# First DFT stage and half-filled depthwise blocks as products on the four quarters of TensorE's array

## The chip, the cores and the metric

The kernel runs on one core of a Trainium2 chip. The metric is the device time of one execution in microseconds; lower is better. TensorE is called PE here, VectorE DVE, ScalarE ACT, GpSimd POOL and SyncE SP, as in the profile.

## The reference

The input is 32 images of 96 channels and 56x56 points, in float32. Two layers follow each other:

- A convolution block: `h = relu(bn(w1 x))` with 576 hidden channels, a 3x3 depthwise convolution on them, again batch norm and ReLU, then `x + bn(w2 h)`.
- On the 3136 tokens of each image: layer norm, `h = relu(bn(w1 t))` with 192 channels, a Fourier transform over the tokens, a complex diagonal product with bias and ReLU on the real and imaginary parts, the inverse transform's real part, a product with `w2`, and the sum with `t`. Then layer norm and a two-layer network of 384 hidden channels whose products are quantized to 8 bits, and the sum with `t`.

```python
X = jnp.fft.fft(h, axis=1, norm='ortho')
xr = relu(X.real * rd - X.imag * idg + rb)
xi = relu(X.imag * rd + X.real * idg + ib)
y = jnp.fft.ifft(xr + 1j * xi, axis=1, norm='ortho').real
```

The transform over 3136 = 56 x 56 tokens is done in two stages of 56 points. This change concerns the first stage, and a part of the depthwise convolution.

## The kernel before

An image is cut into two halves of 28 rows. The 576 hidden channels are four full blocks of 128 and a last block of 64 channels. Each job of the program is a function that makes steps:

- `unit(img, s, k)`, for a half and a full block: PE expands 96 channels to 128 (L582), ACT evicts, DVE runs most of the nine taps (L635), ACT makes one or two taps as products that the POOL queue's DMAs add, ACT applies ReLU (L652).
- `last_channels(img, s)`, for the last 64 channels of a half: the partitions hold 64 channels twice, for even and odd rows, in the tile `hl`. PE does the depthwise convolution itself, as products with `band`, 64x64 diagonal blocks of tap weights. `strip(o, j)` is one of four steps, for the parity `o` of the output row and the slot `j` of the row pair that is read. Each has three column shifts `dc` and two strips of seven row pairs `t`, six matmuls of 128 rows by 64 columns on 7 x 56 points (L727). Output strip `t` lies in the column half 64t of the array. For `j != o` one of the two 64-row blocks of `band` is zero. ACT finishes with ReLU into `al` (L739).
- `front(img, s)` contracts back to 96 channels (L834, L868), keeps the tokens, and starts layer norm. For each of its two quarters of an image `mixer_in` normalizes, turns (L935) and evicts to `xnT` (`turned`, L938), then twice, for four and three of seven groups: `project` (L951), `bend` (ReLU to `z`, L964), `spread` (first DFT stage, L975) and `gather` (copy to `ya`, L986, L990, L991). `send` writes `ya` to `ydr` in DRAM by four DMAs on SP (L1009). In a group 112 partitions hold two image columns of 56 tokens; the matrix `wa` is 112x112 with two 56x56 blocks on its diagonal and zeros elsewhere. There are four `mixer_in` an image.
- `mid(img, half)` loads `ydr` into `yb` (`load`, L1031), does the second DFT stage (L1058), the diagonal product, and the way back to `gdr`, with `half_project` (L1144) and `project` (L1156).
- `back(img, h)` finishes the inverse transform and the quantized network.

All jobs' steps go to one `Plan`. A step names its engine, a cost, the steps it waits for, the buffers that it takes and gives, and a rank. `Plan.emit` runs through time with these costs and sends out, for each engine that is free, the ready step of the lowest rank. So the order of instructions on each engine is fixed when the program is built, and engines work through it in order. `START`, `PACE`, `OFF` and `AT` set ranks; `pe`, `act` and `dve` set costs. Of the buffers, `ps` (PSUM, two banks each) has 3, `z` 2, `ya` 1, `xnT` 1, `hl` one for each half. Their numbers are the counts in `Plan`:

```python
"xt": 1, "norma": 2, "brief": 3, "xnT": 1, "z": 2, "ya": 1, "wb": 1, "yb": 2,
```

Of the kernel before, what the change touches and what calls it, by code (L numbers as in the profile page):

```python
# [46 lines left out]
HF = 384  # L47
SK = 2 * S
NP = S // 2
R = 28  # L50
# [11 lines left out]
def dft_constants():  # L62
# [10 lines left out]
    a1[:, 1, 0] = sign  # L73
    wa = np.zeros((2, S, 2, 2, NP))
    for b in range(2):
        wa[b, :, b] = a1

# [29 lines left out]
    for pair in range(NP):  # L107
# [11 lines left out]
    return {  # L119
        "wa": wa.reshape(SK, SK).astype(np.float32),  # L120
        "wb": wb.reshape(SK, NP * SK).astype(np.float32),
# [7 lines left out]

START = {"last": 9, "front": 7, "mid": 59, "back": 98}  # L130
PACE = {"last": 2.099, "front": 0.4, "mid": 0.675, "back": 0.45}
CHAIN = 0.6

OFF = (-4.0, 1.0, 0.5, 6.5)
AT = (2.5, 1.5)

# [125 lines left out]
def tile_kernel(ctx: ExitStack, tc: tile.TileContext, d: dict, out: bass.AP):  # L262
# [41 lines left out]
    cw = cst([128, 2, 4], "cw")  # L304
    wa = cst([SK, SK], "wa")
    wc = cst([SK, SK], "wc")
# [13 lines left out]
    gd = cst([KD, G, C], "gd")  # L320
    xnT = cst([C + 1, G * SK], "xnT")
    xs_ring = [cst([C, XW], f"xs{j}") for j in range(3)]
# [35 lines left out]
    make_identity(nc, ident)  # L358
    nc.gpsimd.memset(xnT[C : C + 1, :], 1.0)
    nc.gpsimd.memset(band, 0.0)  # L360
# [4 lines left out]
    def loads():  # L365
# [7 lines left out]
        rows = [row(q, n, HA, C + 1) for n in ("a_g1", "a_v1", "a_b1", "a_m1")]  # L373
        load(q, wa, d["wa"])
        yield rows
# [150 lines left out]
    def pe(n, m, passes):  # L526
        return passes * max(0.838 * n, 0.872 * m) / 1000

# [36 lines left out]
    def unit(img, s, k):  # L565
# [95 lines left out]
        for at, q in enumerate(rest):  # L661
            last = q == rest[-1]
            t = step("DVE", dve(W - 28), tap(*q), [t] + c * last, [], ["hs"] * last, rank=4 * n + OFF[2] + at * 3.5 / len(rest))
        if k in DOUBLE:
# [4 lines left out]
    def last_channels(img, s):  # L669
# [44 lines left out]

        def strip(o, j):

            def f():
                if o == j == 0:

                    acc[img, s, NK] = w1.tile([128, RP, S], F32, name="al", bufs=2)  # L720
                    u["d"] = psum()
                pv = u["d"][:, o, 0 : 7 * S].rearrange("p (r c) -> p r c", c=S)
                for dc in (0, -1, 1):
                    ca, cb = max(0, -dc), S - max(0, dc)
                    for t in range(2):
                        at, q = 64 * t, 7 * t + j
                        nc.tensor.matmul(  # L727
                            pv[at : at + 64, :, ca:cb],
                            lhsT=band[:, j, dc + 1, 64 * o : 64 * o + 64],
                            rhs=H[:, q : q + 7, ca + dc : cb + dc],  # L730
                            start=(j == 0 and dc == 0),
                            stop=(j == 1 and dc == 1),
                            skip_group_check=True,
                        )

            return f

        def finish():
# [6 lines left out]

        t = []
        for o in range(2):
            for j in range(2):
                first = ["ps", "al"] if o == j == 0 else []
                t = [step("PE", pe(7 * S, 128, 6), strip(o, j), [a] + t + bands_set, first, [f"hl{s}"] * (o * j))]  # L750
        strips[img, s] = step("ACT", act(14 * S, 1), finish, t, [], ["ps"])
# [64 lines left out]
    def front(img, s):  # L816
# [5 lines left out]
        def conv(i):  # L822

            def f():
                if i == 0:
                    if s == 0:

                        ydr[img] = dram.tile([NP, SK, HA], F32, name="ydr", bufs=4)

                        tdr[img] = dram.tile([2, SK, RP * C], F32, name="tdr", bufs=4)  # L830
                    u["t"] = w1.tile([SK, RP, C], F32, name="xt")
# [62 lines left out]
        for i in range(G):  # L894
            n = min(4, G - i) if i % 4 == 0 else 0
            cost = pe(C, SK, 16) + n * (pe(C, SK, 2) + 0.08)
            if i in (3, 6):
                cost += pe(C, SK, 2 * (i % 4 + 1))
            t = [
                step(  # L900
                    "PE",
                    cost,
                    conv(i),
                    t,
                    ["pw"] * (i % 4 == 0) + ["xt"] * (i == 0) + ["ydr", "tdr"] * (s == 0 and i == 0),
                    (["acc"] * 4 + ["al"]) * (i == G - 1),
                )
            ]
            if i in (3, 6):
                a = i - i % 4  # L910
                ev.append(step("ACT", act((i + 1 - a) * 2 * C), evict(a, i + 1), t, [], ["pw"]))
# [6 lines left out]
    def mixer_in(img, s, j, v, after):  # L918
# [18 lines left out]
        def turned():  # L937
            nc.scalar.activation(  # L938
                xnT[0:C, :].rearrange("p (q w) -> p q w", w=SK), slots(u["ps"])[0:C, 0:G, 0:SK], AF.Copy
            )  # L940
# [4 lines left out]
        def project(i, a, b):  # L945
            def f():
                u["p", i] = psum()
                u["z", i] = w2.tile([SK, 4, HA], F32, name="z")
                pv = u["p", i].rearrange("p j (q w) -> p (j q) w", w=256)
                for q in range(a, b):  # L950
                    nc.tensor.matmul(  # L951
                        pv[0:SK, q - a, 0:HA],
                        lhsT=xnT[:, q * SK : (q + 1) * SK],
                        rhs=watt,
                        start=True,
                        stop=True,
                    )

            return f

        def bend(i, a, b):
            def f():
                pv = u["p", i].rearrange("p j (q w) -> p (j q) w", w=256)
                nc.scalar.activation(u["z", i][:, 0 : b - a, :], pv[0:SK, 0 : b - a, 0:HA], AF.Relu)  # L964

            return f

        def spread(i, a, b):
            def f():
                if i == 0:  # L970
                    u["ya"] = w1.tile([SK, G, HA], F32, name="ya")
                u["y", i] = psum()
                for j, q in enumerate(range(0, b - a, 2)):
                    e = min(q + 2, b - a)
                    nc.tensor.matmul(  # L975
                        u["y", i][0:SK, j, 0 : (e - q) * HA], lhsT=wa, rhs=u["z", i][:, q:e, :], start=True, stop=True
                    )

            return f

        def gather(i, a, b):
            def f():
                ps, ya = u["y", i], u["ya"]
                pv = ps[0:SK, :, 0 : 2 * HA].rearrange("p j (q h) -> p j q h", h=HA)
                if b - a == 4:
                    nc.scalar.activation(  # L986
                        ya[:, a:b, :].rearrange("p (j q) h -> p j (q h)", j=2), ps[0:SK, :, 0 : 2 * HA], AF.Copy
                    )
                else:
                    nc.scalar.activation(ya[:, a : a + 2, :], pv[:, 0, :, :], AF.Copy)  # L990
                    nc.scalar.activation(ya[:, a + 2 : b, :], pv[:, 1, 0 : b - a - 2, :], AF.Copy)  # L991

            return f

        ends = []
        for i, (a, b) in enumerate(HALVES):
            n = b - a
            p = step("PE", pe(HA, SK, 2 * n), project(i, a, b), [t], ["ps", "z"], ["xnT"] * i)
            p = step("ACT", act(n * HA), bend(i, a, b), [p], [], ["ps"])
            p = step("PE", pe(HA, SK, 2 * n), spread(i, a, b), [p] + ends, ["ps"] + ["ya"] * (i == 0), ["z"])  # L1000
            ends = ends + [step("ACT", act(n * HA, 0, 0.05 + 0.05 * i), gather(i, a, b), [p], [], ["ps"])]

        def send():

            yv = ydr[img].rearrange("g (ri b p) h -> ri b g (p h)", ri=2, b=2)
            for b in range(2):
                for ri in range(2):
                    at = b * S + ri * NP
                    nc.sync.dma_start(  # L1009
                        out=yv[ri, b, :, h * G * HA : (h + 1) * G * HA],  # L1010
                        in_=u["ya"][at : at + NP, :, :].rearrange("p q h -> p (q h)"),
                    )
# [4 lines left out]
    def mid(img, half):  # L1017
# [10 lines left out]
        def load(t):  # L1028
            def f():
                u["yb", t] = w2.tile([SK, G, HA], F32, name="yb")  # L1030
                nc.sync.dma_start(  # L1031
                    out=u["yb", t], in_=ydr[img][g0 + G * t : g0 + G * (t + 1)].rearrange("g p h -> p g h")
                )

# [191 lines left out]
    def back(img, h):  # L1226
# [75 lines left out]

        t = step("PE", 0.35, turn, [t], ["ps", "uT"], ["u8"])
        t = step("ACT", act(G * SK), turned, [t], [], ["ps"])
# [37 lines left out]
        for c in range(3):  # L1342
            p = step("PE", 0.35, inner(c), [t], ["ps", "h16"] + ["h8"] * (c == 0), ["uT"] * (c == 2))
            t = p
# [53 lines left out]
        t = step("DVE", 0.34, shift, [t])  # L1398
        t = step("PE", 1.05, total, [t], ["ps", "brief"], ["tt", "y16"])
        t = step("ACT", 0.97, copied_out, [t], [], ["ps"])  # L1400
# [78 lines left out]
```

## Time and profile before

| | us |
|---|---|
| median of 3 runs | 4688.57 (4685.74 to 4690.48) |
| profiled execution, its own time | 4687.61 |
| its span, first to last instruction | 4685.8 |
| PE busy | 4524.5 |
| DVE busy | 4305.0 |
| ACT busy | 4167.4 |
| POOL busy | 339.3 |

The mean granted clock of PE was 0.980. A busy time is the union of an engine's instructions; PE's matmuls are pipelined and their ends are modelled, so what a PE step costs is better read from the start of one step to the start of the next. A float32 matmul of the code is recorded as two instructions ("passes"): L727's 24 matmuls in each of 64 halves are x3072, and L975's four in each of 128 mixers x1024. In a group's row `128*64 128x385` means 128 rows by 64 columns of the array, and 385 moving columns.

### The profile page before, as it was taken

How to read it: one execution, taken by the hardware profiler on the slowest of the kernel's cores; microseconds unless marked ns; L12 is line 12 of the kernel's file. 1: busy time of each engine (PE TensorE's matmuls, PEld its weight loads, DVE VectorE, ACT ScalarE, POOL GpSimd, SP SyncE). 2: the span in 40 equal slices, each digit the busy share in tenths (PEclk: the TensorE clock that was granted, in tenths of full speed). 3: DMA queues.
4: the chain of work that ended last, by engine and by line, in shares of the span. 5: the costliest groups of instructions: out<-in, count | busy, mean ns of one | idle time of the engine just before them, and what ended most of it. 6: DMA issues, size and time to landing. Idle time of an engine off the chain costs nothing.

```text
span 4685.8 us, 83387 instructions
## 1 busy us (share of the span) xinstructions
PE 4524.5 (97%) x32720; PEld 3311.7 (71%) x32720; DVE 4305.0 (92%) x6933; ACT 4167.4 (89%) x5638; POOL 339.3 (7%) x395
## 2 busy tenths in 40 slices
PE   7899999999999999999999999999999999999986
PEld 4566777777777777777777777777777777777774
DVE  8889999999999999999999999999999999999843
ACT  5678899999999999999999999999999999999976
POOL 0100000000000000000000000000000000000000
PEclk7999999999999999999999999999999999999997
DMA  4567876777776777777777777777777777777752
GB/s 96 126 158 164 190 172 168 183 169 176 183 172 170 182 168 177 181 183 165 180 172 175 178 183 171 174 176 173 178 185 167 175 181 170 180 181 167 170 139 78
DMA packets 374994, 789.15 MB, mean 168 GB/s; under 512 B 134052, under 2 KB 234984, under 8 KB 374600
## 3 DMA queue, kind: packets, MB, share of 16 engines
q1 hardware_dynamic: 319144, 479.17, 37.8%
q0 software_dynamic: 55296, 304.64, 33.2%
q8 instruction: 258, 4.23, 0.4%
q14 instruction: 136, 1.11, 0.1%
q10 hardware_dynamic: 160, 0.01, 0.0%
HBM read 286.40 MB, written 192.68 MB: 102 GB/s over the span
## 4 chain that ended last, share of the span: by engine, by line
PE 78%; DMA 8%; ACT 6%; DVE 5%; issue 2%; SPq 0%; ACTq 0%; POOL 0%; DVEq 0%; POOLq 0%
PE pw L834 17%; PE ps L582 13%; DMA gdr<-gc 6%; PE ps L727 6%; PE ps L975 6%; PE ps L951 6%; PE ps L1058 5%; DVE acc L635 3%; PE ps L1257 3%; PE ps L1156 3%; PE ps L1354 2%; PE pw L868 2%; PE ps L684 2%; PE ps L1313 2%; PE ps L935 2%
## 5 line engine op out<-in xcount | busy, mean ns | idle before, releaser
L635 DVE SCALAR_TENSOR_TENSOR acc<-hs,wdw,acc 128x1540 f32<-128x1540 f32 (+2 forms) x1664 | 2972.5, 1794 | 21.9 <-ACT acc L608 9.7
L582 PE MATMUL ps<-xs,w1T 96*128 96x406 f32 x2048 | 821.7, 524 | 15.6 <-ACT hs L592 7.2
L834 PE MATMUL pw<-w2T,acc 128*112 128x96 f32 x7168 | 792.9, 264 | 5.5 <-ACT acc L652 5.4
L834 PEld LDWEIGHTS pw<-w2T,acc 128*112 128x112 f32 x7168 | 755.5, 179 | 50.4 <-issue 26.2
L624 ACT ACTIVATE product<-hs,wdw 128x1568 f32<-128x1568 f32 (+1 forms) x384 | 613.8, 1599 | 15.8 <-DMA product<-product 15.7
L592 ACT ACTIVATE hs<-ps,b 128x812 f32<-128x812 f32 x512 | 482.4, 943 | 153.9 <-PE ps L582 132.4
L727 PE MATMUL ps<-hl,band 128*64 128x385 f32 (+1 forms) x3072 | 551.7, 499 | 2.8 <-ACT hl L707 2.8
L582 PEld LDWEIGHTS ps<-xs,w1T 96*128 96x128 f32 x2048 | 362.5, 192 | 242.9 <-issue 150.8
L643 POOL DMA_DIRECT2D acc<-product x256 | 221.5, 865 | 3646.2 <-DVE acc L635 553.3
L608 ACT ACTIVATE acc<-hs,bd,wdw 128x1568 f32<-128x1568 f32 x256 | 435.3, 1700 | 2.1
L652 ACT ACTIVATE acc<-acc 128x1568 f32<-128x1568 f32 x256 | 386.5, 1510 | 27.2 <-DMA acc<-product 27.1
L727 PEld LDWEIGHTS ps<-hl,band 128*64 128x64 f32 x3072 | 204.7, 137 | 286.7 <-issue 281.6
L1274 ACT ACTIVATE u<-tt,mf,rf 112x96 fp8e5<-112x96 f32 x896 | 347.0, 460 | 10.2 <-DVE mf L810 10.1
L951 PE MATMUL ps<-watt,xnT 97*112 97x192 f32 x1792 | 336.9, 332 | 3.2 <-ACT xnT L938 0.9
L975 PE MATMUL ps<-z,wa 112*112 112x384 f32 (+1 forms) x1024 | 337.0, 451 | 3.1 <-ACT z L964 3.0
L1337 ACT ACTIVATE h<-h 128x784 fp8e5<-128x784 f16 x384 | 331.1, 864 | 9.5 <-DVE h L1331 9.4
L1058 PEld LDWEIGHTS ps<-wb,yb 112*128 112x128 f32 (+1 forms) x3584 | 311.6, 167 | 39.5 <-issue 18.7
L951 PEld LDWEIGHTS ps<-watt,xnT 97*112 97x112 f32 x1792 | 297.1, 179 | 53.0 <-ACT y L1363 18.1
L1058 PE MATMUL ps<-wb,yb 112*128 112x112 f32 (+1 forms) x3584 | 326.1, 272 | 3.6 <-issue 2.3
L1325 ACT ACTIVATE h<-ps 128x784 f16<-128x784 f32 x384 | 315.9, 825 | 9.5 <-PE ps L1313 9.4
L1331 DVE TENSOR_SCALAR h<-h,b1q 128x784 f16<-128x784 f16 x384 | 160.7, 419 | 116.8 <-ACT h L1325 116.3
L975 PEld LDWEIGHTS ps<-z,wa 112*112 112x112 f32 x1024 | 175.3, 177 | 125.2 <-issue 29.2
(148 smaller groups left out, 6514.7 us busy)
## 6 DMA issues: line engine op xcount, KB each, us to landing
acc<-product POOLq DMA_DIRECT2D x256, 784.0 KB, 7.1
product<-product POOLq DMA_DIRECT2D x128, 756.0 KB, 10.6
ydr<-ya SPq DMA_DIRECT2D x512, 147.0 KB
yb<-ydr SPq DMA_DIRECT2D x128, 588.0 KB
wd<-in_wd_dram SPq DMA_DIRECT2D x128, 349.1 KB
wb<-in_wb_dram SPq DMA_DIRECT2D x64, 686.0 KB
xs<-in_x_dram SPq DMA_DIRECT2D x64, 609.0 KB
tdr<-xt SPq DMA_DIRECT2D x64, 588.0 KB
```

The source lines that it names most:

```text
L582: nc.tensor.matmul(u[h][:, j, 0:QW], lhsT=w1T[:, 128 * k : 128 * (k + 1)], rhs=xs[img, s][0:C, at : at + QW], start=True, stop=True,)
L592: nc.scalar.activation(flat[:, 2 * h * QW : 2 * (h + 1) * QW].rearrange("p (j w) -> p j w", j=2), u[h][:, :, 0:QW], AF.Relu, bias=b1[:, k ...
L608: nc.scalar.activation(acc[img, s, k], u["hs"][:, o + up : o + up + R, :], AF.Identity, scale=weight(up, 0), bias=bd[:, k : k + 1],)
L624: nc.scalar.activation(u["p", dr][:, ra:rb, :], u["hs"][:, ra + o + dr : rb + o + dr, :], AF.Copy, scale=weight(dr, 0))
L635: nc.vector.scalar_tensor_tensor(dst, src, weight(dr, dc), dst, ALU.mult, ALU.add)
L652: nc.scalar.activation(acc[img, s, k], acc[img, s, k], AF.Relu)
L727: nc.tensor.matmul(pv[at : at + 64, :, ca:cb], lhsT=band[:, j, dc + 1, 64 * o : 64 * o + 64], rhs=H[:, q : q + 7, ca + dc : cb + dc], star ...
L834: nc.tensor.matmul(u["pw"][0:SK, t, n % 4, 0:C], lhsT=src[rows, (G * t + n) * SK : (G * t + n + 1) * SK], rhs=rhs, skip_group_check=True, **k,
L951: nc.tensor.matmul(pv[0:SK, q - a, 0:HA], lhsT=xnT[:, q * SK : (q + 1) * SK], rhs=watt, start=True, stop=True,)
L975: nc.tensor.matmul(u["y", i][0:SK, j, 0 : (e - q) * HA], lhsT=wa, rhs=u["z", i][:, q:e, :], start=True, stop=True)
L1058: nc.tensor.matmul(o, lhsT=lhsT, rhs=u["wb"][:, G * s + q, :], start=True, stop=True)
L1274: nc.scalar.activation(u["u8"][:, q, :], u["t"][:, q, :], AF.Identity, scale=u["r"][:, q : q + 1], bias=u["m"][:, q : q + 1], saturate=False,)
```

## The change

In `last_channels` four steps become three. `strip(o)` now does the products with `j == o` alone, in which both 64-row blocks are filled. The products with `j != o` are made on the filled 64-row block alone, by a new step `edges`: 12 matmuls of 64 rows by 64 columns, with row half `o` and column half `t`, so that four neighbours in the order lie on the four quarters of the array.

In `mixer_in` both halves are projected and bent first. Then one `spread` does all groups with a 56x64 `wa` that is stored for each row half: the two image columns `b` lie on row halves (partitions 64b to 64b+55), and the first and second part of the groups, `c`, on column halves. It makes 8 matmuls of 384 columns; the second part has three groups, so its first slot is filled with a repeat. Two `gather`s copy 120 partitions by 768. For this `xnT` has 128 columns a group with zeros between its two image columns, `project` uses 120 of them, and `z` and `ya` have 120 partitions. `ydr` is laid out with the real and imaginary parts outermost; `send` writes 56 rows of 768 or 576 numbers in each of its four DMAs, and `load` in `mid` takes two DMAs of 56 partitions instead of one of 112. Some ranks and costs of the plan change. No instruction of DVE is added or removed.

```diff
-START = {"last": 9, "front": 7, "mid": 59, "back": 98}
-PACE = {"last": 2.099, "front": 0.4, "mid": 0.675, "back": 0.45}
+START = {"last": 9, "front": 7, "mid": 62, "back": 98}
+PACE = {"last": 3.023, "front": 0.4, "mid": 0.54, "back": 0.45}
-OFF = (-4.0, 1.0, 0.5, 6.5)
-AT = (2.5, 1.5)
+OFF = (-4.5, 0.5, 0.5, 8.5)
+AT = (3.0, 0.5)
...
-    nc.gpsimd.memset(xnT[C : C + 1, :], 1.0)
+    nc.gpsimd.memset(wa[:, S:], 0.0)
+    nc.gpsimd.memset(xnT[0:C, :, S:64], 0.0)
+    nc.gpsimd.memset(xnT[C : C + 1, :, :], 1.0)
...
-        return passes * max(0.838 * n, 0.872 * m) / 1000
+        return passes * max(0.855 * n, 0.88 * m) / 1000
...
+        def tap(o, j, t, dc, rows=slice(None), **k):
+            pv = u["d"][64 * t : 64 * t + 64, o, 0 : 7 * S].rearrange("p (r c) -> p r c", c=S)
+            ca, cb = max(0, -dc), S - max(0, dc)
+            q = 7 * t + j
+            nc.tensor.matmul(
+                pv[:, :, ca:cb],
+                lhsT=band[rows, j, dc + 1, 64 * o : 64 * o + 64],
+                rhs=H[rows, q : q + 7, ca + dc : cb + dc],
+                skip_group_check=True,
+                **k,
+            )
...
                 for dc in (0, -1, 1):
                     for t in range(2):
+                        tap(o, o, t, dc, start=(dc == 0), stop=False)
...
+        def edges():
+            for dc in (0, -1, 1):
+                for t in range(2):
+                    for o in range(2):
+                        tap(o, 1 - o, t, dc, slice(64 * o, 64 * o + 64), start=False, stop=(dc == 1))
...
-        for o in range(2):
-            for j in range(2):
-                first = ["ps", "al"] if o == j == 0 else []
-                t = [step("PE", pe(7 * S, 128, 6), strip(o, j), [a] + t + bands_set, first, [f"hl{s}"] * (o * j))]
+        t = step("PE", pe(7 * S, 128, 6), strip(0), [a] + bands_set, ["ps", "al"])
+        t = step("PE", pe(7 * S, 128, 6), strip(1), [t])
+        t = [step("PE", pe(7 * S, 128, 6), edges, [t], [], [f"hl{s}"])]
...
+        def spread():
+            u["ya"] = w1.tile([PK, 2, 4, HA], F32, name="ya")
+            for b in range(2):
+                u["y", b] = psum()
+            for j in range(2):
+                for b in range(2):
+                    at = slice(64 * b, 64 * b + S)
+                    for c in range(2):
+                        z = u["z", c]
+                        rhs = z[at, 2 * j - c : 2 * j - c + 2, :] if c == 0 or j else z[at, 0:1, :].to_broadcast([S, 2, HA])
+                        n = 64 - 8 * c
+                        nc.tensor.matmul(
+                            u["y", b][64 * c : 64 * c + n, j, 0 : 2 * HA], lhsT=wa[at, 0:n], rhs=rhs, start=True, stop=True
+                        )
...
             p = step("PE", pe(HA, SK, 2 * n), project(i, a, b), [t], ["ps", "z"], ["xnT"] * i)
-            p = step("ACT", act(n * HA), bend(i, a, b), [p], [], ["ps"])
-            p = step("PE", pe(HA, SK, 2 * n), spread(i, a, b), [p] + ends, ["ps"] + ["ya"] * (i == 0), ["z"])
-            ends = ends + [step("ACT", act(n * HA, 0, 0.05 + 0.05 * i), gather(i, a, b), [p], [], ["ps"])]
+            ends.append(step("ACT", act(n * HA), bend(i, a, b), [p], [], ["ps"]))
+        p = step("PE", pe(2 * HA, 64, 4), spread, ends, ["ps", "ps", "ya"], ["z", "z"])
+        ends = [step("ACT", act(4 * HA), gather(b), [p], [], ["ps"]) for b in range(2)]
...
-            yv = ydr[img].rearrange("g (ri b p) h -> ri b g (p h)", ri=2, b=2)
+            yv = ydr[img].rearrange("ri g (b p) h -> b (ri g) (p h)", b=2)
             for b in range(2):
-                for ri in range(2):
-                    at = b * S + ri * NP
+                for c in range(2):
+                    at = (h * G + 4 * c) * HA
                     nc.sync.dma_start(
-                        out=yv[ri, b, :, h * G * HA : (h + 1) * G * HA],
-                        in_=u["ya"][at : at + NP, :, :].rearrange("p q h -> p (q h)"),
+                        out=yv[b, :, at : at + (4 - c) * HA],
+                        in_=u["ya"][64 * c : 64 * c + S, b, c:4, :].rearrange("p q h -> p (q h)"),
...
-                nc.sync.dma_start(
-                    out=u["yb", t], in_=ydr[img][g0 + G * t : g0 + G * (t + 1)].rearrange("g p h -> p g h")
-                )
+                for ri in range(2):
+                    nc.sync.dma_start(
+                        out=u["yb", t][S * ri : S * (ri + 1), :, :],
+                        in_=ydr[img][ri, g0 + G * t : g0 + G * (t + 1)].rearrange("g p h -> p g h"),
+                    )
```

## The prediction

> **What bounds the kernel now.** I read the page's busy times first, then the windows over the three stages of the run, then the chain and the PE timeline.
>
> ```profile
> span 4685.8 us, 83387 instructions
> PE 4524.5 (97%) x32720; PEld 3311.7 (71%) x32720; DVE 4305.0 (92%) x6933; ACT 4167.4 (89%) x5638; POOL 339.3 (7%) x395
> PE 78%; DMA 8%; ACT 6%; DVE 5%; issue 2%; SPq 0%; ACTq 0%; POOL 0%; DVEq 0%; POOLq 0%
> ```
>
> Three engines are near full, PE the fullest, and 78% of the chain is PE work. An average over the whole run hides the fill and the tail, so I cut it into windows (span, then busy us of PE, PEld, DVE, ACT, POOL, then granted clock, DMA share, GB/s):
>
> ```profile
> 0.00:585.00 585.00, 517.57 (x3303) 361.60 (x3305) 525.42 (x694) 422.01 (x494) 49.15 (x64) 0.92 0.65 147
> 585.00:4446.00 3861.00, 3829.38 (x28184) 2811.24 (x28180) 3681.04 (x5901) 3576.94 (x4857) 290.14 (x331) 1.00 0.74 175
> 4446.00:4686.00 240.00, 177.53 (x1240) 138.86 (x1237) 98.54 (x339) 168.46 (x290) 0.00 (x0) 0.82 0.41 112
> ```
>
> The middle row decides. In 3861 us PE is busy 99.2%, DVE 95.3%, ACT 92.6%: PE sets the pace, and DVE stands only 180 us behind it. One image takes 140.3 us there (the chain shows the same L684 step at 2101.09 and at 2241.37), so the stretch holds 27.5 images. Per image: PE 139.1 us, DVE 133.8, ACT 130.0.
>
> The operations that change, in groups and then in the PE timeline (start, length, passes; a float32 product is recorded as two passes):
>
> ```profile
> L727 PE MATMUL ps<-hl,band 128*64 128x385 f32 x2048 | 378.3, 491 | 0.0
> L727 PE MATMUL ps<-hl,band 128*64 128x392 f32 x1024 | 224.9, 517 | 2.8 <-ACT hl L707 2.8
> L975 PE MATMUL ps<-z,wa 112*112 112x384 f32 x768 | 295.3, 493 | 3.1 <-ACT z L964 3.0
> L975 PE MATMUL ps<-z,wa 112*112 112x192 f32 x256 | 62.4, 325 | 0.0
> ```
>
> ```profile
> 2016.22 1.45 PE L975 MATMUL ps<-z,wa 112*112 112x384 f32 x4
> 2017.51 1.71 PE L1058 MATMUL ps<-wb,yb 112*128 112x112 f32 x14
> ...
> 2020.37 1.72 PE L834 MATMUL pw<-w2T,acc 128*112 128x96 f32 x16
> 2022.02 1.03 PE L868 MATMUL pw<-w2T,al 64*112 64x96 f32 x16
> 2022.98 1.63 PE L582 MATMUL ps<-xs,w1T 96*128 96x406 f32 x4
> 2024.45 1.13 PE L975 MATMUL ps<-z,wa 112*112 112x384 f32 x4
> ```
>
> Lengths overlap, so cost is read from start to start. The first L975 step takes 2017.51 - 2016.22 = 1.29 us for 4 passes of 384 columns (0.322 each). The second (2 passes of 384, 2 of 192) works out to 0.97. L868, on two 64-row halves in turns, needs 0.96 us for 16 passes where L834 needs 1.65 for 16 on the whole array: halves already run side by side. So do L727's two 64-column halves: the chain gives 2.10 us to a step of 12 passes, though each pass is recorded with 0.49, and 4.05 to two steps in a row.
>
> **What the Trainium skill says.** "TensorEngine Tiling (Array Packing)", Key Properties: tiles load weights and multiply independently, and a change of the tiling mode drains the engine. The trace agrees on both for two tiles: the L868 and L727 figures above, and a drain seen as 2 x 2.10 - 4.05 = 0.15 us for one more entry and exit. "TensorE: Matmul & The Clock Gate", Part 3: row and column tiling compose. No run here shows four 64x64 quarters yet; this is the main unknown. The tiling page's Gotcha 1: row tiles must write different PSUM banks. The change does so (output row parity `o` in strips and image half `b` in spread each have a bank of their own). Part 1 of the TensorE page: a PE with idle windows is clocked at half rate. The trace shows 0.92 in the fill and 0.82 in the tail, but still 1.00 between 468 and 585 us, where PE was busy 112.47 of 117 us (96%).
>
> **The change part by part.**
>
> Strips (64 in the run, two an image). Before: four steps of 12 passes, 4 x 2.03 = 8.1 us. The products with band slot j != o use half of the rows alone. After: `strip(0)` and `strip(1)`, 2.03 each, and `edges`, 24 passes on quarters. If four run at once that is 6 rounds of 0.33 us = 2.0. Saved: 2.03, **4.05 us an image**, on PE, which is the path. One switch to quarters comes in, one step goes: even.
>
> Spread (128, four an image). Before 1.29 + 0.97 = 2.26 us. After: 8 products = 16 passes of 384 columns, 4 rounds of 0.322 = 1.29, and a mode entered and left that was not before, 0.15. Saved 0.82, **3.3 us an image**. Of the 16 slots two are repeats of `z` slot 0; they are counted.
>
> PE in all: 4.05 + 3.3 = 7.35 us an image, 5.3% of its work; 202 us in the middle stretch, so PE needs 3829 - 202 = 3627 there.
>
> ACT: three `gather` copies (103.1 + 64.2 + 44.0 = 211.3 us in the run, rows of L986, L990, L991) become two of 768 columns, 256 x 0.805 = 206. Gain 5 us, beside other work. `bend` and `turned` move the same free sizes (0.80 + 0.65, and 0.83). DVE: no instruction added or removed, 6,936 in both orders.
>
> Weights of `project` grow from 112 to 120 columns. Its pace is set by the 192 moving columns (8 passes in 1.32 us on the chain, 0.165 each; L834 shows 0.103 a pass with 112-column weights), so nothing; uncovered, at most 0.007 x 14 passes x 4 = 0.4 us an image.
>
> DMA: `send` still issues four on SP, but 56 rows of 3072 or 2304 bytes in place of 28 of 5376: 112 more pieces a mixer, 14,336 in all. The hardware queue's 37.8% of 16 engines over 319,144 packets is 89 ns each; at that price, too high since the bytes stay, 80 us an engine, under 2% on a share of 74%. `load` in `mid` becomes two DMAs: 128 issues of 0.42 us on SP, 54 us, while SP waits for ACT on `gc` alone 832 us. Behind them in SP's queue stand the later loads; 0.42 us of delay is covered by the wait. At the start one more constant load and two memsets on POOL (a row of 784 took 0.75 us), 1 or 2 us if nothing covered them, taken as nothing.
>
> The added wait: `spread` now waits for both `bend`s and takes two of the three `ps` buffers at once, while before the first half's spread ran when its own `bend` was done. Behind it in PE's fixed order stand products of other images, and ACT waits for those. The planner ranks it later, with other steps between `project` and `spread`. I price the wait at 0; PE's idle time at L975 was 3 us in the whole run, in nearly the same place. If the cover goes, a `bend` takes 0.80 us and two in turn 1.45; times four, 5.8 us an image would be lost.
>
> **What is late next.** PE at 3627 is now below DVE at 3681, with ACT at 3572. So the saving cannot be had whole: DVE becomes the bound. Its floor is 3681 plus the gaps under 0.3 us that even a fed DVE shows; summed over the trace's DVE instructions in this stretch, 31 us: 3712, a gain of 149. With three engines within 3% of one another each waits for the others; PE alone in front reached 99.2%, but three abreast I put at 97.5% for the first: 3681/0.975 = 3775, **86 us less**. The fill was at 90% DVE and the tail has few of these steps: 10 us together (0 to 20). Sum: 96. The profiled execution took 4687.6 (its span 4685.8 and 1.8 around it), the median of three is 4688.6; so 4592. Ends of this case: 4687.6 - 149 - 20 = 4518, and with DVE at 96.2% (35 us gained, the fill none) 4652.
>
> **Rivals.**
> (a) *Waits replace the work*: the two `ps` buffers and the later `spread` give PE bubbles of about 1.5 us per spread, 6 us an image, so all but 1.35 us of the 7.35 go: 27.5 x 1.35 = 37 us gained, 4651, and up to 4690 if the fill and the tail lose as much. For it: three `ps` buffers in all. Against: `half_project` already takes two at once, and L1144 behind it waited 1.2 us in the whole run.
> (b) *Quarters run only two at a time*, slower: then `edges` takes 12 rounds, 3.96 us, and saves nothing, and `spread` 8 rounds, 2.58 + 0.15 = 2.73, is 0.47 slower than before: 128 x 0.47 = 60 us on the bound engine, 4748. It decides from a round of four of 0.59 us in place of 0.32 (with t for the round, an image saves 2 x (4.05 - 6t) + 4 x (2.11 - 4t), which is zero there). For it: never seen here; each float32 product brings two passes for one quarter, which could hold up the queue. Against: the pairs of L727 also have two passes each and still lose nothing. Wholly in turn it would be 24 x 0.33 and 16 x 0.32, above 5000.
> (c) *The clock falls* since PE now idles: at 0.97, PE needs 3627/0.97 = 3739, still under 3775; it takes perhaps 20 us: 4612, inside the first case.
>
> **How the numbers follow.** First case with (c): 0.79, 4592, 4518 to 4652. (a) 0.09, half of it slightly faster, the rest split over no change and slower. (b) 0.10 at 4748, and 0.02 for something worse. Within 0.2% (9 us, about what this measurement can tell from no change) 0.04. Faster 0.83, slower 0.13. The range runs from 4518 to 4680, which takes in most of (a).
>
> **What would show it.** Right: the 24 passes of `edges` last about 2 us from start to start and the 16 of `spread` 1.3 to 1.45; PE busy falls by roughly 200 us in the middle while DVE's share there rises to 97% or more; the image period is near 137 us. Wrong: `edges` near 4 us (b); or short steps with PE idle before L582 or `spread`, named as waiting for ACT on `ps` or `z` (a); or a clock under 0.97 in the middle (c).

## The result and the profile after

The changed kernel takes 4693.35 us in the median of four runs (4682.55 to 4699.67), the kernel before 4687.15 in the same comparison: a ratio of 1.0012, with a 95% interval of 0.9991 to 1.0033. That is no change. The forecast was 4592 us, a gain of 2%. The profiled execution took 4682.55 us, its span 4680.7.

First the page, with the chain of work that ended last in its third line, then the windows over the same stretches as before:

```profile
span 4680.7 us, 85686 instructions
PE 4397.9 (94%) x33744; PEld 3205.3 (68%) x33744; DVE 4299.8 (92%) x6933; ACT 4170.2 (89%) x5510; POOL 337.3 (7%) x397
PE 46%; ACT 14%; DVE 11%; DMA 6%; issue 2%; SPq 0%; POOLq 0%; ACTq 0%; DVEq 0%
```

```profile
0.00:585.00 585.00, 506.78 (x3473) 357.25 (x3474) 536.08 (x709) 429.55 (x491) 49.46 (x67) 0.89 0.65 149
585.00:4446.00 3861.00, 3715.77 (x29058) 2711.43 (x29056) 3667.61 (x5891) 3576.51 (x4744) 287.87 (x330) 0.99 0.73 175
4446.00:4681.00 235.00, 175.36 (x1218) 136.64 (x1216) 96.07 (x334) 164.18 (x278) 0.00 (x0) 0.79 0.39 107
```

PE's work has gone down: 127 us of busy time over the run, 114 in the middle stretch. Nothing took it up. In the middle PE is now busy 96.2%, DVE 95.0% and ACT 92.6%; DVE and ACT stand where they stood before. PE's idle time there rose from 32 us to 145. The chain that ended last was 78% PE; now it is 46% PE, with ACT and DVE in it at 14 and 11. The new shares add up to 79%, because the chain could be followed back only to about 930 us; of the part that was followed PE has some 58%. So the chain changes from engine to engine. The granted clock of PE fell as well, in every stretch.

The quarters themselves do what was forecast. In PE's timeline (start, length, passes) `edges` and one of the `spread`s:

```profile
2055.57 2.18 PE L722 MATMUL ps<-hl,band 64*64 64x392 f32 x24
2057.68 1.20 PE L1369 MATMUL ps<-h,w2q 128*96 128x392 fp8e5 x6
...
2017.07 1.52 PE L994 MATMUL ps<-z,wa 56*64 56x384 f32 x16
2018.51 1.81 PE L844 MATMUL pw<-w2T,acc 128*112 128x96 f32 x16
```

From start to start `edges` takes 2057.68 - 2055.57 = 2.11 us for 24 passes, and `spread` 2018.51 - 2017.07 = 1.44 for 16. Four quarters run at once.

The wait that the change added is in the same timeline, where a bracket gives the idle time before a row and who ended it:

```profile
2064.22 0.86 PE L994 MATMUL ps<-z,wa 56*64 56x384 f32 x4
2065.79 1.50 PE L994 MATMUL ps<-z,wa 56*64 56x384 f32 x12 [0.71 <-ACT hs L594]
```

```profile
PE ps L1369 <- ACT h L1352: 33.1, 24, 3.8
PE ps L963 <- DVE V L1102: 31.4, 25, 2.6
PE ps L994 <- ACT hs L594: 18.2, 20, 2.4
```

The first two matmuls of this `spread` went into one PSUM buffer; the third, which opens the second buffer, had to wait until ACT had emptied it of another unit's expansion. The second fence is the table of waits (total, times, longest). This wait left PE idle 20 times, 18.2 us in the run. That is not all of it: the quarters of the first buffer go on while those of the second one wait, and then no idle time shows. From the first product of a `spread` to the first one into the second buffer, the starts are 58.8 us apart in all, over the 126 of the 128 steps that show both; 58 of them are over 0.1 us late. That is some 1.8 us an image. It is one of many waits, none of which alone explains the missing 2%.

### The profile page after: what moved, and what is told of

It is laid out like the page before. It is cut to its first block, busy times and chain, and to the rows that moved or that the text cites. A ratio compares the mean times of both kernels' runs of the same rounds, so it can differ in the third digit from the quotient of the medians.

```text
span 4680.7 us, 85686 instructions
## 1 busy us (share of the span) xinstructions
PE 4397.9 (94%) x33744; PEld 3205.3 (68%) x33744; DVE 4299.8 (92%) x6933; ACT 4170.2 (89%) x5510; POOL 337.3 (7%) x397
## 4 chain that ended last, share of the span: by engine, by line
PE 46%; ACT 14%; DVE 11%; DMA 6%; issue 2%; SPq 0%; POOLq 0%; ACTq 0%; DVEq 0%
PE pw L844 10%; PE ps L584 8%; DVE acc L637 7%; DMA acc<-product 5%; PE ps L722 4%; PE ps L1073 3%; PE ps L994 2%; PE ps L963 2%; PE ps L1369 2%; PE ps L1272 2%; PE ps L1171 2%; ACT acc L654 2%; PE ps L1328 2%; ACT product L626 1%; ACT acc L610 1%
## 5 line engine op out<-in xcount | busy, mean ns | idle before, releaser
L584 PE MATMUL ps<-xs,w1T 96*128 96x406 f32 x2048 | 823.4, 526 | 48.8 <-ACT al L751 11.6
L844 PEld LDWEIGHTS pw<-w2T,acc 128*112 128x112 f32 x7168 | 766.4, 181 | 64.3 <-issue 40.3
L844 PE MATMUL pw<-w2T,acc 128*112 128x96 f32 x7168 | 804.9, 267 | 5.0 <-ACT acc L654 4.8
L584 PEld LDWEIGHTS ps<-xs,w1T 96*128 96x128 f32 x2048 | 371.2, 195 | 300.0 <-issue 136.0
L594 ACT ACTIVATE hs<-ps,b 128x812 f32<-128x812 f32 x512 | 478.6, 935 | 97.8 <-PE ps L584 83.2
L654 ACT ACTIVATE acc<-acc 128x1568 f32<-128x1568 f32 x256 | 386.9, 1512 | 63.8 <-DMA acc<-product 63.5
L722 PE MATMUL ps<-hl,band 128*64 128x385 f32 (+3 forms) x3072 | 419.3, 498 | 4.5 <-ACT hs L594 2.3
L963 PE MATMUL ps<-watt,xnT 97*120 97x192 f32 x1792 | 350.3, 341 | 44.3 <-DVE V L1102 31.4
L963 PEld LDWEIGHTS ps<-watt,xnT 97*120 97x120 f32 x1792 | 305.2, 190 | 105.4 <-DVE V L1102 40.2
L722 PEld LDWEIGHTS ps<-hl,band 128*64 128x64 f32 (+1 forms) x3072 | 154.7, 135 | 204.1 <-issue 168.8
L994 PE MATMUL ps<-z,wa 56*64 56x384 f32 (+1 forms) x2048 | 242.6, 510 | 24.3 <-ACT hs L594 18.2
L1328 PE MATMUL ps<-uT,w1q 96*128 96x392 fp8e5 x768 | 196.9, 341 | 26.5 <-ACT xnT L948 9.5
```

What stands on the lines that cost most here:

```text
L584: nc.tensor.matmul(u[h][:, j, 0:QW], lhsT=w1T[:, 128 * k : 128 * (k + 1)], rhs=xs[img, s][0:C, at : at + QW], start=True, stop=True,)
L594: nc.scalar.activation(flat[:, 2 * h * QW : 2 * (h + 1) * QW].rearrange("p (j w) -> p j w", j=2), u[h][:, :, 0:QW], AF.Relu, bias=b1[:, k ...
L654: nc.scalar.activation(acc[img, s, k], acc[img, s, k], AF.Relu)
L722: nc.tensor.matmul(pv[:, :, ca:cb], lhsT=band[rows, j, dc + 1, 64 * o : 64 * o + 64], rhs=H[rows, q : q + 7, ca + dc : cb + dc], skip_grou ...
L844: nc.tensor.matmul(u["pw"][0:SK, t, n % 4, 0:C], lhsT=src[rows, (G * t + n) * SK : (G * t + n + 1) * SK], rhs=rhs, skip_group_check=True, **k,
L963: nc.tensor.matmul(pv[0:PK, q - a, 0:HA], lhsT=xnT[:, q, 0:PK], rhs=watt, start=True, stop=True,)
```

## The experiments

**Theories.** (1) The order of instructions, which the planner writes once and every engine follows, sets the time: after the change it has engines waiting for one another in turn, so that none is full. (1b) The half clock takes PE's saving back: PE idles, is clocked down, and needs longer. (2) DVE, now the fullest engine after PE, is the bound. (3) The `spread`'s wait for two of three PSUM buffers is the bound. The plain rival is that PE is still the bound.

| | us, median | ratio to before (95%) | PE clock |
|---|---|---|---|
| changed kernel | 4693.35 | 1.0012 (0.9991 to 1.0033) | 0.967 |
| old plan constants | 4781.14 | 1.0196 (1.0175 to 1.0217) | 0.955 |
| without `edges` | 4722.72 | 1.0062 (1.0047 to 1.0077) | 0.955 |
| without one tap | 4660.15 | 0.9933 (0.9912 to 0.9954) | 0.970 |
| `edges` on all rows | 4764.79 | 1.0151 (1.0128 to 1.0175) | 0.971 |
| changed kernel, reordered | 4570.36 | 0.9748 (0.9734 to 0.9763) | 0.976 |
| kernel before, reordered | 4730.13 | 1.0088 (1.0073 to 1.0103) | 0.981 |
| strips alone | 4780.10 | 1.0197 (1.0172 to 1.0222) | 0.967 |
| first DFT stage alone | 4875.41 | 1.0400 (1.0381 to 1.0419) | 0.960 |
| reordered, without one tap | 4568.63 | 0.9745 (0.9730 to 0.9759) | 0.977 |
| reordered, `edges` on all rows | 4683.66 | 0.9991 (0.9982 to 1.0000) | 0.978 |
| reordered, without `edges` | 4574.38 | 0.9744 (0.9713 to 0.9774) | 0.971 |
| reordered, without both | 4539.46 | 0.9661 (0.9630 to 0.9692) | 0.972 |

**Old plan constants.** The same work, ordered with the constants of before.

```diff
-START = {"last": 9, "front": 7, "mid": 62, "back": 98}
-PACE = {"last": 3.023, "front": 0.4, "mid": 0.54, "back": 0.45}
-OFF = (-4.5, 0.5, 0.5, 8.5)
-AT = (3.0, 0.5)
+START = {"last": 9, "front": 7, "mid": 59, "back": 98}
+PACE = {"last": 2.099, "front": 0.4, "mid": 0.675, "back": 0.45}
+OFF = (-4.0, 1.0, 0.5, 6.5)
+AT = (2.5, 1.5)
# and pe's and dve's costs as before
```

> The changed kernel with the quarter products as they are, but the plan's constants (START, PACE, OFF, AT, and the PE and DVE costs) of the kernel before. The same instructions, in another order. Theory 1, the order made by the planner sets the time, since no engine is full: slower than the changed kernel by 1 to 3%, 4740 to 4830 us. Theory 2, DVE or ACT is the bound as an engine: within 0.5% of the changed kernel, 4670 to 4715 us. Theory 3, the wait of the spread for two of three PSUM buffers sets the time: within 1%.

Measured: 4781.14 us, inside the range of theory 1 and outside those of 2 and 3. Constants that move no work move the time by 1.9%, about as much as the whole gain that was forecast.

**Without `edges`.** The order is left alone; PE loses work: 11 of the 12 products of `edges` are left out, and the sums of the last 64 channels stay incomplete.

```diff
                     for o in range(2):
-                        tap(o, 1 - o, t, dc, ...)
+                        if dc == 0 and t == 0 and o == 0:
+                            tap(o, 1 - o, t, dc, ...)
```

> The changed kernel in the same order, but the step edges makes one of its 12 products (the depthwise sums of the last 64 channels are left incomplete): some 64 x 1.9 = 120 us of PE work less. Theory 1 (order and waits between the engines): under 40 us faster, 4650 to 4695 us. Theory 1b, the half clock gives PE's savings back: no gain either, and the granted clock falls further, to 0.955 or less. Rival, PE is still the bound: 80 to 120 us faster, 4575 to 4610 us.

Measured: 4722.72 us. The work taken away is 81 us and not 120: from start to start all strip and edge products of the run take 407.7 us in the changed kernel and 326.7 here, as the one product that stays takes some 0.9 us alone. With that much less to do the program is slower than the changed kernel (ratios 1.0062 and 1.0012, intervals that do not meet), and the clock is down to 0.955. PE's work as the bound is out. Theory 1b had said no gain and a clock of 0.955 or less, and both came; that it would even be slower no theory had said. The same stretch, 585 to 4320 us, of the changed kernel and of this one:

```profile
585.00:4320.00 3735.00, 3594.24 (x28096) 2622.64 (x28095) 3551.88 (x5697) 3461.09 (x4586) 279.10 (x320) 0.99 0.73 175
```

```profile
585.00:4320.00 3735.00, 3545.06 (x26729) 2594.60 (x26726) 3518.48 (x5655) 3434.58 (x4546) 278.31 (x318) 0.98 0.73 174
```

PE's idle time rises from 141 to 190 us, and the clock falls from 0.99 to 0.98: 1% of 3735 us is some 37 us of PE time lost there.

**Without one tap.** DVE loses work, a tenth of it: one of the nine taps of every unit is left out.

```diff
-                nc.vector.scalar_tensor_tensor(dst, src, weight(dr, dc), dst, ALU.mult, ALU.add)
+                if (dr, dc) != (0, -1):
+                    nc.vector.scalar_tensor_tensor(dst, src, weight(dr, dc), dst, ALU.mult, ALU.add)
```

> The changed kernel in the same order, but every unit leaves out one of its depthwise taps on DVE (column shift -1 in the same row): 256 x 1.73 = 443 us of DVE work less, 10%. Theory 1 (order and waits): under 100 us faster, 4600 to 4690 us. Theory 2 (DVE is the bound): DVE's floor falls to 3860 us, so PE or ACT must bind next: 200 us faster or more, 4490 us or less.

Measured: 4660.15 us, some 33 us less than the changed kernel, for 418 us less of DVE's busy time (4299.8 to 3881.9). DVE as an engine is not the bound; theory 2 is out.

**`edges` on all rows.** PE gets the work back that the quarters of the strips had saved.

```diff
-                        tap(o, 1 - o, t, dc, slice(64 * o, 64 * o + 64), start=False, stop=(dc == 1))
+                        tap(o, 1 - o, t, dc, start=False, stop=(dc == 1))
```

> The changed kernel in the same order, but edges uses all 128 rows again, the zero half included: its 24 passes then run two at a time, 4.05 instead of 2.1 us, 64 x 1.95 = 125 us of PE work given back. Theory 1: PE's idle time takes up most of it, under 60 us slower, 4690 to 4750 us. Rival, PE is still the bound: 100 to 125 us slower, about 4810 us.

Measured: 4764.79 us, 71 more than the changed kernel for 125 us of work. That lies between the two ranges. So PE's steps are on the path in places. A reading that fits this run and the one without `edges`: a step that becomes longer shifts what follows, while one that becomes shorter leaves a gap, since the next in line waits for another engine.

**Reordered.** The decisive experiment: every instruction of the changed kernel, in another order.

```diff
-START = {"last": 9, "front": 7, "mid": 62, "back": 98}
-PACE = {"last": 3.023, "front": 0.4, "mid": 0.54, "back": 0.45}
-AT = (3.0, 0.5)
+START = {"last": 8.5, "front": 7, "mid": 62, "back": 98}
+PACE = {"last": 3.627, "front": 0.3845, "mid": 0.5416, "back": 0.45}
+AT = (5.0, 1.0)
...
-            t = step("DVE", dve(W - 28, 0.16), tap(*q), ...
+            t = step("DVE", dve(W - 28, 0.1), tap(*q), ...
```

> The changed kernel, the same instructions in another order: START last 8.5, PACE last 3.627, front 0.3845, mid 0.5416, AT (5, 1), and 0.10 us for the fixed part of a DVE tap in the plan's costs. The set was found by replaying orders with the step times that the traces of before and after show, which puts an image at 133.0 us instead of 137 to 139. Theory 1 (order): 90 to 170 us faster than the changed kernel, 4520 to 4600 us, and DVE busy 97% or more of the middle. Rival, the gain is held back by something no order can lift (DMA, half clock, contention): 4650 us or more.

Measured: 4570.36 us, 2.5% faster than the kernel before. This version beats both. Its window from 585 to 4320 us:

```profile
585.00:4320.00 3735.00, 3650.97 (x28898) 2662.76 (x28899) 3644.19 (x5862) 3550.03 (x4714) 286.82 (x329) 1.00 0.75 180
```

PE is busy 97.8%, DVE 97.6%, ACT 95.0%, and the clock is back at 1.00. What has changed is how regularly the images follow. ACT's timeline shows one eviction of `hl` for each half; every second one, in the changed kernel and then in the reordered one:

```profile
2100.18 0.91 ACT L705 ACTIVATE hl<-ps,b 128x784 f32<-128x784 f32 x1
...
2240.67 0.91 ACT L705 ACTIVATE hl<-ps,b 128x784 f32<-128x784 f32 x1
...
2385.69 0.90 ACT L705 ACTIVATE hl<-ps,b 128x784 f32<-128x784 f32 x1
...
2525.31 0.91 ACT L705 ACTIVATE hl<-ps,b 128x784 f32<-128x784 f32 x1
```

```profile
2121.78 0.90 ACT L705 ACTIVATE hl<-ps,b 128x784 f32<-128x784 f32 x1
...
2257.89 0.90 ACT L705 ACTIVATE hl<-ps,b 128x784 f32<-128x784 f32 x1
...
2393.93 0.90 ACT L705 ACTIVATE hl<-ps,b 128x784 f32<-128x784 f32 x1
...
2529.32 0.90 ACT L705 ACTIVATE hl<-ps,b 128x784 f32<-128x784 f32 x1
```

The images are 140.5, 145.0 and 139.6 us apart in the first, 136.1, 136.0 and 135.4 in the second.

The order itself shows the difference more sharply. Take PE's steps, by their lines, from each such eviction to the next. In the kernel before and in the reordered one this sequence is exactly the same for every image from the sixth on: the planner has settled into a repeating order. In the changed kernel no two neighbouring images have the same sequence; in the middle some 78% of the steps agree, laid side by side as well as they fit. With the old plan constants it is 60%; with the strips alone and the first DFT stage alone, which follow below, it is 61 and 66%.

**The kernel before, reordered**, as a fair counterpart.

```diff
-OFF = (-4.0, 1.0, 0.5, 6.5)
-AT = (2.5, 1.5)
+OFF = (-4.0, 0.5, 0.5, 11.0)
+AT = (3.0, 3.0)
...
-        return passes * max(0.838 * n, 0.872 * m) / 1000
+        return passes * max(0.845 * n, 0.88 * m) / 1000
...
-            cost = pe(C, SK, 16) + n * (pe(C, SK, 2) + 0.08)
+            cost = pe(C, SK, 16) + n * (pe(C, SK, 2) + 0.13)
```

> The kernel before, the same instructions in another order: OFF (-4, 0.5, 0.5, 11), AT (3, 3), PE costs 0.845 and 0.88, 0.13 for the start of a group in front. It was the best found in the same way. Theory 1: PE needs 136 us an image by its measured step times and bounds this form, so an order can give little: 4630 to 4680 us. Rival, the kernel before was held back by its order just as much: under 4600 us, and then the quarters give nothing of their own.

Measured: 4730.13 us, a miss by theory 1's numbers: 0.9% slower than the order it had. The replay that chose this order was 50 us and more too hopeful here. The rival, under 4600, is further off. This order repeats too, from the seventh image on, so a repeating order alone is not yet a good one. The best order of the old form that was run stays its own, with PE busy 99.2% in the middle; that none is better is not shown.

**Each half of the change alone**, with the constants of before: `last_channels` of the changed kernel in the kernel before, and then `mixer_in`, `send` and `load` in it.

```diff
# strips alone
-        t = []
-        for o in range(2):
-            for j in range(2):
-                first = ["ps", "al"] if o == j == 0 else []
-                t = [step("PE", pe(7 * S, 128, 6), strip(o, j), ...)]
+        t = step("PE", pe(7 * S, 128, 6), strip(0), [a] + bands_set, ["ps", "al"])
+        t = step("PE", pe(7 * S, 128, 6), strip(1), [t])
+        t = [step("PE", pe(7 * S, 128, 6), edges, [t], [], [f"hl{s}"])]
# first DFT stage alone: the other parts of the change, these four lines as before
```

> The kernel before with the quarter products of last_channels alone, its plan's constants unchanged: 64 x 2.1 = 134 us of PE work less than before. Theory 1: the old constants fit the old steps, the new ones fall out of the repeating order, 4740 to 4840 us, slower than before. Rival, PE's saving counts: 4560 to 4640 us.

> The kernel before with the quarter products of the first DFT stage alone, its plan's constants unchanged: 128 x 0.82 = 105 us of PE work less, and the spread that waits for both halves and takes two PSUM buffers. Theory 1: out of the repeating order, 4770 to 4850 us. Theory 3, the wait for the two PSUM buffers is what eats the gain: slower than strips alone by 50 us or more, with PE idle before the spread. Rival, PE's saving counts: 4590 to 4650 us.

Measured: 4780.10 and 4875.41 us. The strips alone wait for nothing new and use no more PSUM, take some 133 us of work from PE, and cost 2.0%; theory 3 can't explain that, theory 1 can. The first DFT stage alone costs 4.0%, 25 us beyond what was expected for theory 1. It is 95 us slower than the strips, as theory 3 asks; but theory 3 also asks that PE stand idle before the `spread`, and it hardly does. The group of that product in this run, its idle time after the second bar:

```profile
L986 PE MATMUL ps<-z,wa 56*64 56x384 f32 x1024 | 228.8, 503 | 11.6 <-ACT o L1396 5.6 <-ACT uT L1303 2.3 <-ACT hs L594 1.1
```

PE is idle 11.6 us before the `spread`, and the products into the second buffer start late by 37 us in all, in a program that is 185 us slower than the kernel before. Theory 3 in its plain form falls. That holding two buffers delays other users of PSUM, which then wait elsewhere, isn't excluded.

**What binds the good order?** The same three edits on the reordered kernel, and two of them together.

> The reordered changed kernel (4570 us) in its order, with the same one tap of DVE left out in every unit: 256 x 1.73 = 443 us of DVE work less. If DVE as an engine is what bounds the good order (it is busy 97.6% there), 70 to 130 us are gained until PE and ACT bind, 4440 to 4500 us. If the fixed order with its waits binds here too, about 40 us, as in the order given with the change: 4520 to 4540 us.

> The reordered changed kernel in its order, with edges on all 128 rows: 64 x 1.95 = 125 us of PE work given back. If DVE bounds the good order, PE's slack takes most of it: under 50 us slower, 4570 to 4620 us. If PE's steps lie on the path, 70 to 125 us slower, 4640 to 4695 us.

> The reordered changed kernel in its order, with one of the 12 products of edges alone (sums of the last 64 channels incomplete): some 120 us of PE work less, as in the second run, but in the good order. If PE's steps are the path there, 50 to 110 us faster, 4460 to 4520 us. If idle windows and the half clock take back what PE saves, as in the order given with the change, no gain or slower, 4560 to 4610 us, with a granted clock under 0.97.

> The reordered changed kernel in its order, with both left out: 11 of 12 products of edges (120 us of PE work) and one DVE tap in every unit (443 us). Either alone gave nothing. If PE and DVE bound it together, each hiding the other, 50 to 110 us faster, 4460 to 4520 us. If a third thing stands at 136 us an image (ACT, its DMA-added products, or chains through all engines in the fixed order), under 30 us faster, 4540 to 4580 us.

Measured: without the tap 4568.63 us, no gain from 418 us less of DVE's busy time; either theory had forecast at least 30. With `edges` on all rows 4683.66, 113 us more for 125 us of PE work: PE stands close to the bound here. Without `edges` (79 us less work from start to start) 4574.38 us, no gain either; the clock fell to 0.971, but not under the 0.97 named. Without both 4539.46 us, 31 less, just past the edge of the range for a third thing at 136 us an image. That third thing is not found: ACT, the DMA-added products that it waits for, or chains through all engines remain. There is a lead. The chain that ended last, by lines, in the reordered kernel and in the one without both:

```profile
DMA acc<-product 11%; DVE acc L637 9%; PE pw L844 9%; PE ps L584 6%; PE ps L722 5%; PE ps L963 4%; PE ps L1073 3%; ACT acc L610 3%; ACT acc L654 3%; ACT h L1352 3%; PE ps L994 2%; ACT hs L594 2%; ACT ya L1000 2%; PE ps L1369 1%; PE ps L945 1%
DMA acc<-product 11%; PE pw L846 9%; DVE acc L638 7%; PE ps L584 6%; PE ps L965 3%; PE ps L1075 3%; ACT acc L610 3%; ACT acc L655 3%; ACT u L1291 3%; PE ps L723 2%; ACT h L1354 2%; PE ps L996 2%; ACT product L626 2%; ACT hs L594 2%; ACT ya L1002 2%
```

The transfer that adds a product to `acc` stands first in all five runs of this order except those without the tap alone and without `edges` alone, where it is second, always with about 11%; it had 1% of the span before the change and 5% after it. No run changed it, so that it binds is not shown. What is shown is that DVE's 97.6% is not what binds, and that in either order taking work from one engine gives little or nothing.

## Why the prediction was wrong

**Bound before**: right. PE set the pace, and `edges` on all rows costs nearly its full length where the order is good.

**Saving on PE**: right for a step that nothing disturbs, too large for the run. `edges` takes 2.11 us (said: 2.0), and a strip step standing alone 2.10, so a half of an image saves about 2.1 us; an undisturbed `spread` takes 1.44, as said, and saves 0.82. Rival (b), two at a time, is refuted: where the page "TensorEngine Tiling (Array Packing)" of the Trainium skill says in Key Properties that tiles work independently, the trace agrees for four 64x64 quarters of float32, with 24 passes in 2.11 us. But 7.35 us an image would be 235 us in 32 images, and PE's busy time fell by 127. From start to start, idle time left out, the strips save 133 us in the run (said: 130), `spread` 62 (said: 105), `project` takes 21 more (said: nothing), and the remaining steps, which did not change, take some 47 more at the lower clock. In the reordered kernel PE's busy time fell by 174.

**What is late next**: this is the step that failed. "Three abreast I put at 97.5% for the first" is a share of busy time that DVE did not reach: 95.0% was measured. It took the order of instructions for something that adapts. It does not: it is written when the program is built, from ranks and costs, and the order that came with the change kept DVE near its 95.3% of before and brought PE down to 96.2%. In another order the same instructions reach 97.6% and 4570 us, 22 us from the number forecast. So the number 97.5% is met in a good order, and the error lay in granting it to this one. That it is met there is partly luck, since its reason, that DVE becomes the bound, also fell: a tenth of DVE's work less changes nothing there.

**The added wait, priced at 0**: 18.2 us of idle time in the table of waits, and 58.8 us by the late starts, some 1.8 us an image; in the reordered kernel the late starts come to 32 us. So a price of nothing was wrong. The mechanism of rival (a) exists, and its end, about 4690 us, is where the kernel came out; but that is luck: the PE bubbles are spread over many places, not some 6 us an image at the `spread`, and the strips alone, with the constants of before, lose time without that wait.

**The clock**, rival (c): 0.99 in the middle instead of 1.00, inside what (c) allowed, and 0.967 in all instead of 0.980; 1.3% of the span is 61 us of PE time. It was taken for a cost of 20 us beside a gain. It belongs to the lost gain. Three programs with the same instructions bound its part: reordered, changed and with the old constants they have clocks of 0.976, 0.967 and 0.955, and PE is busy 4350.2, 4397.9 and 4450.3 us in them. So of the 114.5 us between the spans of the first two at most 48 are the same PE work taking longer, and 67 are more idle time. What causes what was not separated: no run held the one and changed the other, and in the reordered kernel's middle PE was idle less (84 us instead of 141 in the 3735) while the clock was at 1.00.

**Nothing for DMA, SP and the wider weights**: DVE's and ACT's busy times are the same to within 0.2%, as said. But `project`, with the wider weights, takes 19 us more in the reordered kernel too, where the clock was nearly that of before; the prediction's ceiling for it, 0.4 us an image or 13 us, is nearer than its nothing. And ACT's wait for the transfers that add products rose from 27.1 to 63.5 us, though the same numbers are moved; the order sets when they are asked for, and whether that is the reason is not shown.

## What to carry to other kernels

Where the order on each engine is fixed ahead of time, work taken off the fullest engine is worth what the new order makes of it, and an edit that changes a step's length or number is also an edit of the order. Judge such an edit only with an order found anew for it, and look whether the sequence of steps repeats from image to image, and how evenly equal steps are spaced. Here no order that does not repeat was faster than the kernel before with all of its work done; one order of the kernel before that does repeat was slower too, so this is a first check and no proof. Three engines at 95% each are no sign that one of them is the bound; take work from one in the same order, and see.

## What the hardware showed that was not expected

Less work can cost time: without `edges` PE had 81 us less to do, and the program took 29 us more than the changed kernel (4722.72 against 4693.35), at a granted clock of 0.955 instead of 0.967. A PE that is busy 95% of the time in the middle still had its clock lowered there, to 0.98; at 97.8%, in the good order, it had 1.00. The busy share alone does not set it: with the old plan constants PE was busy 95.4% in the same stretch and had 0.97. A wait of two of the four quarters need not show as idle time of PE: of the 58.8 us of late starts in `spread`, some 15 show as idle time within the steps.

Short pauses came before the half clock. From 585 to 4320 us the clock was halved 15 times in the changed kernel, for 82 us in all, 31 times for 167 us without `edges`, and once in the kernel before and in the reordered one. One such place in the changed kernel, PE's busy time and clock just before and after:

```profile
2130.30:2137.10 6.80, 5.28 (x37) 1.00 0.39 106
2137.10:2143.90 6.80, 6.80 (x34) 0.50 0.27 89
```

PE was idle for 1.5 of the 6.8 us before, the longest pause was 0.97 us, and that pause was a `spread` waiting for its second buffer. Then the clock was halved, and 16 passes of L844 that take 1.7 us elsewhere took 3.3. If that pause lowered the clock, which is not shown, the wait cost more than its own length. How short a pause is enough, these runs do not tell.
